# A three-sublayer decoder block on one core: the last pair's output sum, norm and store in two halves, and a new table of starting places for the order

## The chip, the cores and the metric

One Trainium2 chip, one of its cores, one launch. The metric is the device time in microseconds (us) of one execution. All arithmetic is in float32.

## The reference

A batch of 16 sequences of 256 tokens with 256 channels goes through three sublayers, each added to its input and layer-normed:

```python
x = _layernorm(x + attn(x, ...))        # scan-type attention: projections, conv, sin/cos, cumsums
x = _layernorm(x + xattn(x, ctx, ...))  # auto-correlation: DFT of q and k, top-5 lags, roll of v
x = _layernorm(x + ffn(x, ...))         # two branches of 8 experts with a router
```

In the last one, with `xV = Q @ V_k`, `cum_yW = cumsum(K @ W_k)` along the tokens and router weights `w`:

```python
out = einsum('btkr,kdr->btd', xV * cum_yW * w[..., None], U) + w @ b
out = out / n_valid                      # then fwd + alpha * inv, times W_O.T
```

## The kernel before, in words

The 16 sequences are worked on in 8 pairs. For each pair the program lists seven stages: `front` (in-projection, convolution, gates), `body` (sin, cos, cumulative sums, out-projection, first norm), `context` and `back` (keys and values of the second sublayer, kept in HBM between the two), `attention` (second sublayer and norm), `router` and `experts` (third sublayer). `fold_weights` multiplies weights with each other once, ahead of the pairs (`w_ps`).

No instruction is issued as it is listed. Class `Later` records every call as an `Op`; then `Work.run` lays out an order for all five engines, and `Work.give` issues it. So nearly all instructions carry the one line L452, and table loads of ScalarE L450. The layout is a list schedule: each engine takes, of the operations that can go, the one with the lowest rank. It is made three times (`PASSES`). In the first pass a rank is `place(part)`, which is `begin[pair] + part * length` of the stage's row in the table `PLACES`; in the next passes it is the latest start found by going back through the layout before. The shortest of the three layouts by the planner's own costs is issued. `Work.note` finds which operation must wait for which; for PSUM, the memory that TensorE writes, `Work.box` takes a bank as a whole: two operations on different columns of one bank are taken to meet.

```python
    def place(stage, pair, part):
        length, *begin = PLACES[stage]
        return begin[pair] + part * length
```

A change of a few numbers in `PLACES`, or of the list of operations, can thus move instructions of all pairs on all engines.

`experts(p)`: eight expert blocks make `e` (128 x 512: 128 rows, 2 x 256 tokens) from two matmul groups `c_ps` and `v_ps`; the router's weights come in as `wb` through a DMA. Then `u_ps`: for each token half `c` (tokens 0 to 127, then 128 to 255) and each sequence `j` of the pair, 8 matmuls with `u_o` and one with the bias `b_o`. There are two banks, `banks[j]`, one for each sequence; columns 0 to 255 of a bank hold half `c = 0`, columns 256 to 511 half `c = 1`. At the end VectorE adds each bank to `x` (128 x 512), `layernorm` takes four tiles of 128 x 256 (statistics on VectorE, square root and scaling on ScalarE), and GpSimd issues one store of 256 KB for each sequence.

Names in the profile: `sc_ps`, `in_ps` belong to `front`; `y`, `ss`, `out_ps` to `body`, `sn` and `cs` being its sine and cosine tiles; `dft_ps` on `bothc` and `kv_ps` to `context`; `dft_ps` on `dx`, `q_ps`, `corr_ps`, `w_t_ps`, `w_f_ps`, `roll_ps`, `wo_ps` to `attention`; `fx_ps`, `h_ps`, `l_ps`, `lt_ps`, `wt_ps` to `router`.

Of the kernel before, what the change touches and what calls it, by code (L numbers as in the profile page):

```python
# [16 lines left out]
ALU = mybir.AluOpType  # L17
# [4 lines left out]
P = 128  # L22
# [10 lines left out]
NP = B // 2  # L33
# [3 lines left out]


PLACES = {
    "front": (1.0, 1.75, 3.7, 4.05, 4.2, 5.15, 5.65, 6.15, 8.0),  # L40
    "body": (0.5, -1.2, 1.45, 3.3, 1.4, 4.5, 4.55, 6.85, 7.75),
    "ctx": (0.9, 2.18, 0.8, 1.3, 1.6, 1.9, 1.3, 1.55, 2.55),
    "back": (0.5, -2.85, -2.95, -4.9, -5.5, -1.75, -3.0, -1.2, 2.1),
    "att": (0.1, -1.95, -2.75, -2.4, -4.5, -0.05, 0.45, 1.4, 4.15),
    "router": (1.45, 0.9, -3.2, 2.15, 2.1, 2.9, 4.65, 5.9, 4.9),
    "expert": (1.18, 4.05, 3.55, 5.65, 5.85, 7.4, 6.9, 9.8, 12.25),
    "fold": (2.75, 2.21),
}
EARLY, SLABS, XT_BUFS, ZC_BUFS, KBUFS, VBUFS, X_BUFS = 3, 17, 1, 4, 2, 3, 9
AHEAD = range(1, NP)  # L50
# [63 lines left out]
class Work:  # L114
# [67 lines left out]
    @staticmethod  # L182
# [3 lines that stand above are left out]
# [270 lines left out]
def decoder_kernel(ctx: ExitStack, tc: tile.TileContext, a: dict, out: bass.AP):  # L456
    nc = tc.nc
    ctx.enter_context(tc.manual_schedule())
    work = Work(0.1)
    work.scalar = nc.scalar  # L460
    work.shares.update({"raw": 11, "inv": 2, "ks": 6, "ct": 2, "bothc": 1, "specc": 2, "e": 8, "wb": 3, "h": 2, "lT": 1, "lg8": 1, "fwT": 2, "x": 3, "dx": 2, "x2": 4})
    V, S, G, T, Y = (
        Later(work, name, eng)
        for name, eng in (
            ("DVE", nc.vector), ("ACT", nc.scalar), ("POOL", nc.gpsimd), ("PE", nc.tensor), ("SP", nc.sync)
        )
    )
# [7 lines left out]
    ff = ctx.enter_context(tc.tile_pool(name="ff", bufs=1))  # L475
# [13 lines left out]
    def new(pool, shape, tag, bufs=1, name=None):  # L489
        work.apart()  # L490
        return pool.tile(shape, F32, name=name or tag, tag=tag, bufs=bufs)

    def slab(shape, name):
        return new(ff, shape, "slab", SLABS, name)
# [4 lines left out]
    def f_bank(name):  # L499
        return new(f_ps, [P, 512], "fps", 4, name)  # L500

    def split(ps, n=2):
        return ps.rearrange("p (c d) -> p c d", c=n)
# [70 lines left out]
    def layernorm(pool, tag, tiles, eps=None):  # L574
        n = len(tiles)
        st = new(pool, [P, n, 6], tag + "st")
        mv = new(pool, [P, n, 2], tag + "mv")
        rs = new(pool, [P, 3, n], tag + "rs")
        for i, t in enumerate(tiles):
            V.bn_stats(st[:, i, :], t)  # L580
            V.bn_aggr(mv[:, i, :], st[:, i, :])
        t, y, nb = (rs[:, i, :] for i in range(3))
        S.activation(t, mv[:, :, 1], AF.Sqrt, bias=b_eps if eps is None else eps)
        V.reciprocal(y, t)
        V.scalar_tensor_tensor(nb, mv[:, :, 0], -1.0, y, ALU.mult, ALU.mult)
        for i, t in enumerate(tiles):
            S.activation(t, t, AF.Identity, scale=y[:, i : i + 1], bias=nb[:, i : i + 1])
# [196 lines left out]
    ps = f_bank("bv_ps")  # L784
# [362 lines left out]
    def copies(wT, kb):  # L1147

        return wT.rearrange("(n k) t -> n k t", k=KEXP)[:, kb].unsqueeze(1).to_broadcast([16, 8, 512])

    def experts(p):
        place = lambda f: work.place("expert", p, f)
        xT, cT = inputs.pop(p)
        pair = (xs[2 * p], xs[2 * p + 1])
        es = []
        for kb in range(8):
            cut = slice(kb * P, (kb + 1) * P)
            work.rank = place(kb * 0.08)
            early = kb < EARLY
            e = slab([P, 512], "e")  # L1160
            if not early:
                wb = slab([P, 512], "wb")
                Y.dma_start(out=wb, in_=copies(routed[p], kb))
            ps = f_bank("c_ps")
            for c in range(2):
                T.matmul(ps, w_c[:, c, cut], cT[:, c, :, :], start=c == 0, stop=c == 1)
            if early:
                S.copy(e, ps)
            else:
                V.tensor_tensor(e, wb, ps, ALU.mult)  # L1170
            ps = f_bank("v_ps")
            for c in range(2):
                T.matmul(ps, w_v[:, c, cut], xT[:, c, :, :], start=c == 0, stop=c == 1)
            V.tensor_tensor(e, e, ps, ALU.mult)
            es.append(e)
        wT = routed.pop(p)
        for kb in range(EARLY):
            wb = slab([P, 512], "wb")
            Y.dma_start(out=wb, in_=copies(wT, kb))
            V.tensor_tensor(es[kb], es[kb], wb, ALU.mult)  # L1180
        banks = [None, None]
        for c in range(2):
            for j in range(2):
                work.rank = place(0.65 + 0.1 * c + 0.05 * j)
                if c == 0:
                    banks[j] = f_bank("u_ps")
                work.apart()
                o, cut = banks[j][:, c * D : (c + 1) * D], slice((2 * j + c) * P, (2 * j + c + 1) * P)
                for n, i in enumerate([*range(EARLY, 8), *range(EARLY)]):
                    T.matmul(o, es[i][:, cut], u_o[:, i, :], start=n == 0, stop=False)  # L1190

            work.apart()
            work.joins = True
            for j in range(2):
                rows, cut = slice(64 * j, 64 * j + 64), slice((2 * j + c) * P, (2 * j + c + 1) * P)
                T.matmul(banks[j][:, c * D : (c + 1) * D], wT[rows, cut], b_o[rows, :], start=False, stop=True)
            work.joins = False
            work.apart()
        tiles = []
        for j in range(2):  # L1200
            V.tensor_tensor(pair[j], pair[j], split(banks[j]), ALU.add)
            tiles += [pair[j][:, 0, :], pair[j][:, 1, :]]
        work.rank = place(1.0)
        layernorm(ff, "fl", tiles)
        for j in range(2):
            G.dma_start(out=out[2 * p + j].rearrange("(c p) d -> p c d", p=P), in_=pair[j])

    fold_weights()
    for p in range(NP):
        for stage in (front, body, context, back, attention, router, experts):  # L1210
            stage(p)
# [138 lines left out]
```

## Time and profile before

| what | us |
|---|---|
| median of 3 timed runs (lowest, highest) | 867.02 (865.38, 867.68) |
| the profiled execution, its own time | 862.73 |
| its span, first to last instruction | 861.0 |
| TensorE busy in it | 811.5 |
| VectorE busy | 695.2 |
| ScalarE busy | 596.2 |
| GpSimd busy | 254.3 |

The profiled execution is one execution; its time holds 1.73 us outside the span. Busy time of TensorE (PE) is that of pipelined matmuls whose ends are modelled; PEld is its weight load; DVE is VectorE, ACT ScalarE, POOL GpSimd, SP the engine that issues most DMAs. The span falls into three parts: a beginning (to about 55 us) in which weights are fetched, folded and the first pair's chain starts; a long middle in which two to three pairs are under way at once; and an end, from about 785 us, in which only the last pair's `router` and `experts` are left.

### The profile page before, as it was taken

To read this page: it belongs to the slowest core of one execution; us is meant where nothing else is said; L and a number is where in the kernel's file an instruction comes from. 1 tells how busy PE (TensorE), PEld (TensorE's weight loads), DVE (VectorE), ACT (ScalarE), POOL (GpSimd) and SP (SyncE) were. 2 spreads that over 40 slices of the span, in tenths; PEclk is the share of its full clock that TensorE was granted. 3 is DMA by queue.
4 is the path that set the end of the run, shared out by engine and by line. 5 is a ranking of instruction groups with operands and counts; after the bars stand their busy time and mean duration, and the time that the engine had idled before them with its cause. 6 is when DMAs were issued, how large, how long until landed. Compare 5 with 4: busy or idle time off the path is not lost.

```text
span 861.0 us, 12052 instructions
## 1 busy us (share of the span) xinstructions
PE 811.5 (94%) x4180; PEld 462.2 (54%) x4180; DVE 695.2 (81%) x1200; ACT 596.2 (69%) x874; POOL 254.3 (30%) x301
## 2 busy tenths in 40 slices
PE   4779998999989999999998999999999999999994
PEld 1336564564546654764453746655457357548453
DVE  6479799879899999999999799988979994472431
ACT  2769968699897999599668956769388932712601
POOL 8501456551512132433220312434122111221000
PEclk9879999999999999999999999999999999999997
DMA  7952787374745336535484436336351711130040
GB/s 232 346 129 51 191 246 200 124 198 111 187 105 143 81 87 168 130 71 142 100 181 96 116 78 146 106 86 158 76 133 39 186 34 50 44 80 1 24 98 25
DMA packets 57421, 103.30 MB, mean 120 GB/s; under 512 B 7616, under 2 KB 24032, under 8 KB 57360
## 3 DMA queue, kind: packets, MB, share of 16 engines
q1 hardware_dynamic: 47760, 71.85, 35.6%
q0 software_dynamic: 9600, 30.69, 10.9%
q8 instruction: 33, 0.54, 0.3%
q14 instruction: 28, 0.23, 0.1%
HBM read 28.06 MB, written 11.53 MB: 46 GB/s over the span
## 4 chain that ended last, share of the span: by engine, by line
PE 63%; ACT 13%; DVE 9%; issue 6%; DMA 5%; POOL 2%; SPq 1%; POOLq 0%; DVEq 0%; ACTq 0%
PE u_ps L452 11%; PE v_ps L452 9%; PE c_ps L452 9%; PE h_ps L452 5%; PE kv_ps L452 4%; PE in_ps L452 4%; PE w_ps L452 3%; PE wo_ps L452 3%; ACT L450 3%; DVE cs L452 3%; PE y L452 2%; ACT cs L452 2%; PE ss L452 2%; PE out_ps L452 2%; DVE sn L452 2%
## 5 line engine op out<-in xcount | busy, mean ns | idle before, releaser
L450 ACT ACT_TABLE_LOAD x101 | 129.6, 1283 | 1.8
L452 PE MATMUL v_ps<-fxT,w_v 128*128 128x512 f32 x256 | 121.0, 602 | 2.6 <-DVE e L452 1.2
L452 PE MATMUL c_ps<-fcT,w_c 128*128 128x512 f32 x256 | 120.1, 601 | 0.1
L452 PE MATMUL u_ps<-u_o,e 128*128 128x256 f32 x512 | 116.4, 382 | 0.0
L452 PEld LDWEIGHTS u_ps<-u_o,e 128*128 128x128 f32 x512 | 95.6, 190 | 19.1 <-issue 6.7
L452 DVE TENSOR_TENSOR_SCAN cs<-again,cs 128x1024 f32<-128x1024 bf16 x32 | 77.3, 2417 | 0.0
L452 PEld LDWEIGHTS v_ps<-fxT,w_v 128*128 128x128 f32 x256 | 46.2, 190 | 54.1 <-issue 42.8
L452 DVE TENSOR_TENSOR_SCAN sn<-again,sn 128x1024 f32<-128x1024 bf16 x32 | 74.6, 2332 | 0.1
L452 PEld LDWEIGHTS c_ps<-fcT,w_c 128*128 128x128 f32 x256 | 46.5, 190 | 50.2 <-issue 46.8
L452 DVE SCALAR_TENSOR_TENSOR zc<-in_ps,pv,zc 128x510 f32<-128x510 f32 (+2 forms) x96 | 69.3, 734 | 1.6 <-ACT zc L452 1.1
L452 PE MATMUL h_ps<-fxT,w_h 128*128 128x512 f32 x128 | 61.4, 619 | 4.0 <-ACT fxT L452 4.0
L452 PE MATMUL in_ps<-xT,in_proj_w 128*128 128x512 f32 x128 | 62.6, 619 | 2.0 <-DVE sc L452 2.0
L452 PE MATMUL kv_ps<-Wkv,specc 128*128 128x512 f32 x128 | 61.3, 612 | 3.2 <-ACT specc L452 2.9
L452 POOL TENSOR_TENSOR pp<-qf,kf 128x256 f32<-128x256 f32 (+1 forms) x32 | 43.7, 1383 | 69.3 <-ACT qf L452 64.7
L452 DVE TENSOR_TENSOR e<-e,v_ps 128x512 f32<-128x512 f32 x64 | 43.0, 674 | 14.5 <-PE v_ps L452 14.4
L452 POOL DMA_DIRECT2D out<-x x16 | 11.7, 730 | 135.5 <-ACT x L452 123.1
L452 ACT ACTIVATE sn<-sn,theta_col 128x512 f32<-128x512 f32 x64 | 44.6, 714 | 9.0 <-DMA sn<-zc 8.8
L452 POOL TENSOR_TENSOR t<-vf,wf 128x256 f32<-128x256 f32 x32 | 22.8, 732 | 92.0 <-ACT wf L452 49.7
L452 DVE SCALAR_TENSOR_TENSOR cs<-cs,sn 128x1024 f32<-128x1024 f32 x32 | 42.1, 1315 | 9.3 <-ACT cs L452 9.1
L452 DVE TENSOR_TENSOR sn<-sn,ge 128x1024 f32<-128x1024 f32 x32 | 41.4, 1295 | 6.6 <-ACT sn L452 3.7
L452 ACT ACTIVATE ge<-sn 128x1024 f32<-128x1024 f32 x32 | 33.7, 1053 | 17.0 <-DVE sn L452 9.6
L452 ACT ACTIVATE zc<-in_ps,pv 128x512 f32<-128x512 f32 x32 | 24.6, 778 | 30.1 <-PE in_ps L452 30.1
(220 smaller groups left out, 1600.5 us busy)
## 6 DMA issues: line engine op xcount, KB each, us to landing
sn<-zc SPq DMA_DIRECT2D x64, 256.0 KB
ge<-g SPq DMA_DIRECT2D x64, 256.0 KB
wb<-fwT SPq DMA_DIRECT2D x64, 256.0 KB
ct<-in_ctx SPq DMA_DIRECT2D x16, 256.0 KB
xT<-in_xT SPq DMA_DIRECT2D x8, 512.0 KB
x<-in_x POOLq DMA_DIRECT2D x16, 256.0 KB, 3.9
ph<-sc SPq DMA_DIRECT2D x64, 64.0 KB
gate<-zc SPq DMA_DIRECT2D x64, 64.0 KB
```

The lines of the kernel that those rows point to most:

```text
L450: self.scalar.preload_act_table_set(self.TABLES[table])
L452: call(*args, **kw)
```

## The change

Two things. In `experts`, for the last pair alone (`p == NP - 1`), the add, the layernorm and the store are listed once for each token half, right behind that half's matmuls, on 128 x 256 tiles; the other pairs keep one add, norm and store behind both halves, now with the adds ranked at `place(1.0)` too. And all eight rows of `PLACES` have other numbers.

```diff
 PLACES = {
-    "front": (1.0, 1.75, 3.7, 4.05, 4.2, 5.15, 5.65, 6.15, 8.0),
-    "body": (0.5, -1.2, 1.45, 3.3, 1.4, 4.5, 4.55, 6.85, 7.75),
-    "ctx": (0.9, 2.18, 0.8, 1.3, 1.6, 1.9, 1.3, 1.55, 2.55),
-    "back": (0.5, -2.85, -2.95, -4.9, -5.5, -1.75, -3.0, -1.2, 2.1),
-    "att": (0.1, -1.95, -2.75, -2.4, -4.5, -0.05, 0.45, 1.4, 4.15),
-    "router": (1.45, 0.9, -3.2, 2.15, 2.1, 2.9, 4.65, 5.9, 4.9),
-    "expert": (1.18, 4.05, 3.55, 5.65, 5.85, 7.4, 6.9, 9.8, 12.25),
-    "fold": (2.75, 2.21),
+    "front": (1.05, 1.75, 3.2, 4.1, 4.35, 5.8, 5.7, 6.05, 8.5),
+    "body": (0.6, -1.0, 1.65, 3.5, 1.75, 4.5, 3.85, 6.75, 8.2),
+    "ctx": (0.85, 2.88, 0.0, 2.0, 2.15, 4.15, 1.95, 2.15, 3.45),
+    "back": (2.6, -3.7, -2.4, -4.8, -5.75, -1.4, -2.85, -2.3, 2.85),
+    "att": (2.1, -6.05, -6.25, -7.35, -9.0, -5.1, -2.85, -2.25, 2.15),
+    "router": (1.15, 2.5, -2.35, 3.8, 3.2, 4.25, 5.1, 7.65, 5.65),
+    "expert": (0.98, 4.45, 3.9, 5.85, 5.8, 8.3, 7.75, 9.95, 13.3),
+    "fold": (4.45, 2.76),
 }
...
             work.joins = False
             work.apart()
-        tiles = []
-        for j in range(2):
-            V.tensor_tensor(pair[j], pair[j], split(banks[j]), ALU.add)
-            tiles += [pair[j][:, 0, :], pair[j][:, 1, :]]
-        work.rank = place(1.0)
-        layernorm(ff, "fl", tiles)
-        for j in range(2):
-            G.dma_start(out=out[2 * p + j].rearrange("(c p) d -> p c d", p=P), in_=pair[j])
+
+            if p == NP - 1 or c == 1:
+                halves = [c] if p == NP - 1 else [0, 1]
+                work.rank = place(1.0)
+                for j in range(2):
+                    x, ps = pair[j][:, halves[0] : c + 1, :], split(banks[j])[:, halves[0] : c + 1, :]
+                    V.tensor_tensor(x, x, ps, ALU.add)
+                layernorm(ff, "fl", [pair[j][:, h, :] for j in range(2) for h in halves])
+                for j in range(2):
+                    rows = out[2 * p + j].rearrange("(c p) d -> p c d", p=P)[:, halves[0] : c + 1, :]
+                    G.dma_start(out=rows, in_=pair[j][:, halves[0] : c + 1, :])
```

## The prediction

> **What bounds the kernel now.** I read the page's busy times and slices first, then TensorE's waits, then the end's timeline, then the first 75 us engine by engine. Busy times and slices, one digit for 21.5 us:
>
> ```profile
> PE 811.5 (94%) x4180; PEld 462.2 (54%) x4180; DVE 695.2 (81%) x1200; ACT 596.2 (69%) x874; POOL 254.3 (30%) x301
> PE   4779998999989999999998999999999999999994
> DVE  6479799879899999999999799988979994472431
> PEclk9879999999999999999999999999999999999997
> ```
>
> TensorE is the bound: 811.5 of 861.0 us, full from the fourth slice to the last but one. Both orders hold the same matmuls, so the time can only fall by what TensorE idles (49.5 us) or does at a lower clock. VectorE is nearly full too from about 220 to 460 us, and has room after 700. TensorE's waits, with total, count and longest in us:
>
> ```profile
> PE sc_ps L452 <- DMA xT<-in_xT: 15.7, 2, 8.8
> PE h_ps L452 <- ACT fxT L452: 4.0, 2, 3.1
> PE w_ps L452 <- ACT vf L452: 3.4, 1, 3.4
> PE kv_ps L452 <- ACT specc L452: 2.9, 2, 1.9
> PE w_f_ps L452 <- ACT wT L452: 2.0, 1, 2.0
> PE wt_ps L452 <- POOL lg L452: 1.8, 1, 1.8
> ```
>
> All waits of this view sum to 37.7 us; the other 11.3 us are the end, from TensorE's last matmul (849.70) to 861.0. Its timeline:
>
> ```profile
> 841.90 7.17 PE L452 MATMUL u_ps<-u_o,e 128*128 128x256 f32 x32
> 849.00 0.70 PE L452 MATMUL u_ps<-b_o,fwT 64*128 64x256 f32 x4
> 849.73 1.28 DVE L452 TENSOR_TENSOR x<-x,u_ps 128x512 f32<-128x512 f32 x2 [14.58 <-PE u_ps L452]
> 850.94 0.74 DVE L452 BATCH_NORM_STATS2 flst<-x 128x6 f32<-128x256 f32 x2
> ...
> 853.52 2.07 ACT L452 ACTIVATE x<-x,flrs 128x256 f32<-128x256 f32 x4 [0.44 <-DVE flrs L452]
> 854.90 0.72 POOL L452 DMA_DIRECT2D out<-x  x1 [39.09 <-ACT x L452]
> 855.89 0.72 POOL L452 DMA_DIRECT2D out<-x  x1 [0.26 <-ACT x L452]
> ```
>
> Nothing overlaps TensorE here: add, statistics, scaling, store, in that order. The sum below is made against the profiled execution's 862.73 us; the median of the timed runs is 4.3 us above it, and I carry the difference over unchanged.
>
> **Part 1, the end.** From the last matmul to the second store's issue before: 849.70 to 855.89, 6.19 us. For the last half after: two adds of 128x256 for 0.75 (the bias add of that shape took 0.42, and the second overlaps), two statistics instead of four (1.74 us for the group, so 0.87), the square root chain 0.84 as before, two scalings instead of four, the first store after one of them (0.52 + 0.35), the second 0.98 behind it, the spacing of the two stores above. 0.75 - 0.04 + 0.87 + 0.84 + 0.87 + 0.98 = 4.27. Gain 1.9; GpSimd's issue, not ScalarE, sets it. The last store moves 128 KB instead of 256 KB; at the 351 to 359 GB/s that the DMA view shows for the old ones, 0.3 less. Together **-2.2** (bounds -2.6, if stores do not space, to -1.2, if only adds and statistics shrink). The first half's chain, some 5.2 us with its stores, lies beside the 7.87 us of matmuls of the second half; without that cover it would give back all of this. Only two more stores on GpSimd's queue come of it, with nothing queued behind.
>
> The Trainium skill (DMA: Bandwidth & Descriptors, Anatomy of one DMA) fits a store from GpSimd as a fixed 2.0 us and bytes over 436 GB/s; by it halving the bytes saves an estimated 0.3 us and the rest of the landing stays, which the trace's rates agree with.
>
> **Part 2, a new wait at the end.** Both halves of a sequence lie in one bank and the planner takes a bank as a whole, so in the built program the second half's first matmuls wait for VectorE's add of the first. Queued behind it on TensorE are the second half's 36 matmuls, and the whole end. No row shows it. Lower bound: the add's 0.42 plus the 0.03 by which an add follows its matmul, 0.45. Upper: that plus a window at half clock, 1.7, so 2.2. The two waits of 0.64 and 0.91 us near 680 us left the clock at 1.00, so I take **+0.5**.
>
> **Part 3, the beginning.** The orders part after 13 matmuls. Before, TensorE waited 6.91 us for the second pair's `xT`, which SP had issued at 36.45 behind `ge` and `ph`; 3.44 for a ScalarE copy of `vf`; 1.05 for `f_dft`. After, SP issues that `xT` and all of `ph` ahead of `ge`, and GpSimd the folding weights ahead of `f_dft` and `Wkv`: these 11.4 us can go. But the first pair's chain then decides. VectorE ended its fourth scan at 59.1 us and TensorE used it at 61.6: only 2.5 us of room. TensorE has 3.4 us more work placed ahead of it (rows' durations). Against that, `ge` now stands on SP behind one `gate` copy, whose source ScalarE finished at 34.2 us: it goes out some 6.6 us later (28.2 to 34.8), of which 4.7 come back since VectorE no longer waits 4.68 us for the second `ph`. -2.5 - 3.4 + 1.9 = -4.0 if all of it lasts, 0 if the work placed ahead only leaves less for later waits. I take the middle, **-2**; bounds -6 and +4 (`ge` late by 6.6 with 2.5 of room).
>
> **Part 4, the middle.** The changed table moves instructions on all engines; only TensorE's last 292 matmul calls of 2154 stand as before, some 131 us of work. I counted, in both built orders, how much matmul work (0.86 us for a pair of 128x512, 0.43 for 128x256, and so on from the rows) stands between a group and the group that needs its result; little work between is a wait. From `fx_ps` to `h_ps`, pairs 1 to 7: 0.9, 0.9, 2.1, 0.0, 1.7, 1.8, 2.2 before, never under 1.7 after; the 0.0 is the 3.1 us wait. From `w_t_ps` to `w_f_ps`: lowest 0.0 before (the 2.0 us wait), 1.7 after. From `lt_ps` to `wt_ps`, pairs 1 to 6: lowest 6.1 before (the 1.8 us wait), 9.7 after. So 4.0 + 2.0 + 1.8 = 7.8 us go. After the 3.1 us wait the clock was low:
>
> ```profile
> 452.00:455.00 3.00, 0.59 (x5) 0.35 (x3) 2.97 (x3) 3.00 (x5) 0.00 (x0) 1.00 0.92 273
> 455.00:458.00 3.00, 2.33 (x3) 1.08 (x4) 3.00 (x3) 2.98 (x5) 0.00 (x0) 0.63 0.00 0
> ```
>
> (the first figure behind the comma is TensorE's busy time, the third from the end the granted clock). 0.37 x 3.0 = 1.1 us more. The Trainium skill (TensorE: Matmul & The Clock Gate, Part 1) puts the clock back to half only after an idle window of about 3.4 us; by that this wait of 3.08 us would have cost no clock and the sum would lack the 1.1, but the row shows 0.63, so the trace does not agree.
>
> New waits: from `dft_ps` to `kv_ps` five of 16 places have under 1 us after (one of them in the beginning), one before. The two waits there cost 2.9 us, 1.44 each; four give 5.8, so +2.9. From `dft_ps` on `dx` to `q_ps` one place has 0.9 instead of at least 1.7: +0.9, as long as the 0.9 us wait at an `h_ps` with 0.9 between. Together -7.8 - 1.1 + 3.8 = **-5.1** (bounds -10, no new wait, to +4, all old waits replaced).
>
> ScalarE has 14 table loads fewer (88 for 102, the first load included), 18.0 us by the row's 1283 ns. ScalarE is idle 265 us, so I count them at nothing beside the waits above; that is a rival's matter.
>
> **Part 5, VectorE in the middle.** By rows' durations the order after has 2 to 7 us (mean 4.8) more VectorE work ahead of the scans that feed `y` of the third and fourth pair, while TensorE's work ahead is the same within 0.4 in the mean. Before, the last three `y` groups of the third pair followed their scans by 0.0 to 0.8 us (one scan ends at 249.6, its `y` starts at 249.68). The 4.7 us that VectorE no longer waits for `ph` nearly cover it: **+0.1** (bounds 0 and +7).
>
> **Sum.** -2.2 + 0.5 - 2.0 - 5.1 + 0.1 = -8.7 us: 862.73 becomes 854.0 for a profiled execution, and the median 867.02 becomes **858.3**. A measurement of this kernel can tell about 0.3%, 2.6 us, from no change.
>
> **Rivals.** *VectorE takes over (slower).* Between 220 and 460 us VectorE is busy 97%; each wait that TensorE loses then comes back at `y`, nothing is kept of parts 3 and 4, and the scan with most work ahead sets the delay, 7.3 x 0.92 = 6.7 us (my VectorE durations add to 757 for 695 busy). 6.7 - 1.7 = +5.0: 872.0. It decides if VectorE's idle time ahead of 240 us, 44 us now, falls by less than about 2. For it: the gaps of 0.0 to 0.8. Against: the `ph` stall, and 12 of the 14 loads saved lie ahead of the first pair's last norm, so VectorE should wait less for ScalarE early.
>
> *Only the end counts.* Waits in the middle are traded one for one, as the new places at `kv_ps` suggest: -2.2 + 0.5, 865.3, no change to be told.
>
> *Table loads matter.* Line L450 has 3% of the chain that ended last, 25.8 us for 101 loads, 0.26 each; 14 fewer give -3.6 on top of the sum: 854.7. For it: several loads lie in the chain between 140 and 260 us. Against: part 4 has counted some of these waits already.
>
> **Numbers.** The forecast gets 0.55, with its own range 853 to 864; table loads 0.15; only the end 0.10; VectorE 0.20. Faster by over 0.3% is the first two, 0.70; the same 0.10; slower 0.20. The range goes from 850 (part 3 at its best under the table loads) to 871.5, just short of the rival's 872.0; some 2 in 10 stay outside.
>
> **What would show it.** Right: the last matmul to the end of the span 9.1 us instead of 11.3, a TensorE wait on VectorE's add of about 0.5 between the halves, `sc_ps` on `xT` waiting only once for long, no wait of over 1 us at `h_ps`, `w_f_ps`, `wt_ps`. Wrong: waits of `y` on `cs` or `sn` that add up to over 5 us, a long wait for `ge` before the first `y`, or a clock below 1.00 in the last 8 us of matmuls.

## The result, and the profile after

| | median, us (lowest, highest) | ratio to before, 95% |
|---|---|---|
| before, in this comparison | 866.53 (865.38, 867.68) | |
| the changed kernel | 861.80 (860.40, 862.63) | 0.9957 [0.9939, 0.9975] |
| the changed kernel, in the next comparison | 862.10 (860.64, 866.17) | 0.9977 [0.9960, 0.9994] |

So the change is faster, by 0.2 to 0.4%: by the ratios 3.7 us in the first comparison (the medians differ by 4.7) and 2.0 us in the second (before's median there: 864.54, of 35 executions). The forecast was 8.7 us, 1.0%. The two profiled executions show less still: 862.73 us before, 862.63 after, spans 861.0 and 860.8. Executions of one kernel differ here by more than the effect (before: 861.3 to 869.3 us in those 35), so single traces are used below for where TensorE waits, and medians for what it is worth.

Busy times and slices of the changed kernel, one digit for 21.5 us:

```profile
PE 810.6 (94%) x4180; PEld 463.0 (54%) x4180; DVE 698.5 (81%) x1204; ACT 580.6 (67%) x861; POOL 267.6 (31%) x303
PE   4598999899979999999999989999999999999995
DVE  5589689988999999999989989998888894563341
PEclk9899999999999999999999999999999999999998
```

TensorE's work is unchanged and so, nearly, is its idle time. Its waits (total, count, longest, in us):

```profile
PE sc_ps L452 <- DMA xT<-in_xT: 18.0, 2, 9.1
PE y L452 <- DVE cs L452: 3.6, 5, 1.5
PE kv_ps L452 <- DVE ks L452: 3.4, 1, 3.4
PE kv_ps L452 <- ACT specc L452: 3.3, 2, 1.9
PE y L452 <- DVE sn L452: 2.9, 1, 2.9
PE wt_ps L452 <- POOL lg L452: 1.4, 1, 1.4
PE c_ps L452 <- DVE x L452: 1.2, 1, 1.2
```

The view sums to 41.0 us, against 37.7 before. The rows that the prediction wanted gone are gone (`h_ps`, `w_f_ps` but 0.2 us, `w_ps` on `vf`) except `wt_ps`, and the rows above on `y`, on `ks` and on `x` are new or longer. Between 62 us and the last half of matmuls, counting waits of 0.25 us and more, 15.1 us before became 17.3. The end:

```profile
843.73 0.75 DVE L452 TENSOR_TENSOR x<-x,u_ps 128x256 f32<-128x256 f32 x2 [6.85 <-PE u_ps L452]
844.21 7.17 PE L452 MATMUL u_ps<-u_o,e 128*128 128x256 f32 x32 [0.51 <-DVE x L452]
851.31 0.70 PE L452 MATMUL u_ps<-b_o,fwT 64*128 64x256 f32 x4
852.04 0.75 DVE L452 TENSOR_TENSOR x<-x,u_ps 128x256 f32<-128x256 f32 x2 [5.90 <-PE u_ps L452]
855.39 1.07 POOL L452 DMA_DIRECT2D out<-x  x2 [7.19 <-ACT x L452]
```

From TensorE's last matmul (852.01) to the end of the span it is 8.8 us, 11.3 before; the second half waits 0.51 us for VectorE's add of the first. That is 2.0 us gained, where Parts 1 and 2 had 1.7 (-2.2 and +0.5). But the last matmul itself comes at 852.01 instead of 849.70: beginning and middle together lost 1.8 us in this execution, the 0.51 us apart.

### The profile page after: what moved, and what is told of

The parts are those of the page before. It is cut to its first block, busy times and chain, and to the rows that moved or that the text cites. A ratio compares the mean times of both kernels' runs of the same rounds, so it can differ in the third digit from the quotient of the medians.

```text
span 860.8 us, 12074 instructions
## 1 busy us (share of the span) xinstructions
PE 810.6 (94%) x4180; PEld 463.0 (54%) x4180; DVE 698.5 (81%) x1204; ACT 580.6 (67%) x861; POOL 267.6 (31%) x303
## 4 chain that ended last, share of the span: by engine, by line
PE 66%; DVE 11%; issue 7%; ACT 7%; DMA 6%; POOL 1%; SPq 1%; POOLq 0%; DVEq 0%; ACTq 0%
PE u_ps L452 12%; PE v_ps L452 10%; PE c_ps L452 9%; PE h_ps L452 5%; PE kv_ps L452 4%; PE in_ps L452 4%; PE out_ps L452 3%; PE wo_ps L452 3%; PE q_ps L452 3%; DVE cs L452 3%; PE y L452 2%; PE dft_ps L452 2%; DVE sn L452 2%; PE ss L452 2%; DMA ge<-g 2%
## 5 line engine op out<-in xcount | busy, mean ns | idle before, releaser
L452 PE MATMUL c_ps<-fcT,w_c 128*128 128x512 f32 x256 | 120.6, 603 | 2.0 <-DVE x L452 1.2
L452 PE MATMUL v_ps<-fxT,w_v 128*128 128x512 f32 x256 | 119.9, 600 | 0.0
L452 PE MATMUL u_ps<-u_o,e 128*128 128x256 f32 x512 | 116.8, 382 | 0.5 <-DVE x L452 0.5
L452 PEld LDWEIGHTS u_ps<-u_o,e 128*128 128x128 f32 x512 | 95.5, 190 | 19.4 <-issue 6.0
L452 DVE TENSOR_TENSOR_SCAN cs<-again,cs 128x1024 f32<-128x1024 bf16 x32 | 79.2, 2475 | 0.0
L452 PEld LDWEIGHTS c_ps<-fcT,w_c 128*128 128x128 f32 x256 | 47.1, 191 | 57.2 <-issue 47.7
L452 DVE TENSOR_TENSOR_SCAN sn<-again,sn 128x1024 f32<-128x1024 bf16 x32 | 75.2, 2351 | 0.1
L452 PEld LDWEIGHTS v_ps<-fxT,w_v 128*128 128x128 f32 x256 | 46.7, 190 | 52.0 <-issue 45.5
L452 DVE SCALAR_TENSOR_TENSOR zc<-in_ps,pv,zc 128x506 f32<-128x506 f32 (+2 forms) x96 | 69.7, 734 | 3.4 <-ACT zc L452 2.8
L452 PE MATMUL kv_ps<-Wkv,specc 128*128 128x512 f32 x128 | 63.4, 630 | 6.7 <-DVE ks L452 3.4
L452 PE MATMUL in_ps<-xT,in_proj_w 128*128 128x512 f32 x128 | 63.4, 622 | 2.1 <-DVE sc L452 2.1
L452 POOL TENSOR_TENSOR pp<-qf,kf 128x256 f32<-128x256 f32 (+1 forms) x32 | 46.8, 1482 | 46.7 <-ACT qf L452 43.0
L452 PE MATMUL h_ps<-fxT,w_h 128*128 128x512 f32 x128 | 59.3, 601 | 0.1
L452 DVE TENSOR_TENSOR e<-e,v_ps 128x512 f32<-128x512 f32 x64 | 42.9, 674 | 15.4 <-PE v_ps L452 15.3
L452 POOL TENSOR_TENSOR t<-vf,wf 128x256 f32<-128x256 f32 x32 | 22.2, 714 | 97.1 <-ACT wf L452 51.6
L452 DVE TENSOR_TENSOR sn<-sn,ge 128x1024 f32<-128x1024 f32 x32 | 44.2, 1382 | 8.3 <-DMA ge<-g 5.3
L452 POOL TENSOR_TENSOR g<-g,zc 128x512 f32<-128x512 f32 x16 | 24.8, 1550 | 82.4 <-ACT g L452 82.4
L452 ACT ACTIVATE sn<-sn,theta_col 128x512 f32<-128x512 f32 x64 | 44.8, 715 | 7.6 <-DMA sn<-zc 7.5
L452 ACT ACTIVATE ge<-sn 128x1024 f32<-128x1024 f32 x32 | 33.8, 1056 | 22.6 <-DVE sn L452 13.6
L452 POOL DMA_DIRECT2D out<-x x18 | 12.5, 693 | 116.8 <-ACT x L452 116.5
L452 ACT ACTIVATE sq<-cs 128x1024 f32<-128x1024 f32 x32 | 33.8, 1055 | 17.1 <-DVE cs L452 16.5
```

The lines of the kernel that those rows point to most:

```text
L452: call(*args, **kw)
```

## The experiments

All but after_again and before_again, which are the two kernels unchanged, hold the order of the instructions fixed: the list that the planner issued is written into the kernel, and parts of it are changed. (Their instructions then carry the line L588 instead of L452.) "Old order" is that of before, "new order" that of the changed kernel.

```diff
-    work.run(PASSES)
+    work.give([work.ops[int(k)] for k in ORDER], None)
```

### The two halves of the change, each alone, and both kernels again

split_alone: old order, end in halves. order_alone: new order, whole end.

```diff
-ORDER = old order, one add, norm and store at the end
+ORDER = old order up to the last pair's adds, then the halves  # split_alone
+ORDER = new order up to there, one add, norm and store         # order_alone
```

> The order of the kernel before, kept instruction by instruction; only the last pair's add, norm and store are done in two halves. If the end is worth what the two profiles show (last matmul to end of the span 11.3 us before, 8.8 after, and a new wait of 0.5 us): 2.0 us faster than before. If the measured 4.7 us come mostly from the split: 4 us or more. If the end counts for nothing: within 0.5 us of before.

> The order of the changed kernel, kept instruction by instruction; the last pair's add, norm and store are one piece as before. If the new order is worth the rest of the measured 4.7 us: 2.7 us faster than before. If VectorE takes over what TensorE no longer waits for (TensorE's waits add up to 41.0 us in the changed kernel's profile, 37.7 in the old one's): the same as before or up to 3 us slower. If the prediction's parts 3 to 5 hold: 7 us faster.

> The changed kernel once more, for the spread of its executions: if its profiled execution (860.8 us of span) was an ordinary one, another profile has a span of 859 to 861 and the same waits within 1 us each.

> The kernel before once more: its profiled execution took 862.73 us, its timed ones 865.38 to 867.68. If the profiled one was a lucky one, this profile has a span of 864 to 866 and some waits are longer than in the first; if profiled executions are faster than others as such, the span is again 861.

| run | median, us | ratio to before, 95% |
|---|---|---|
| split_alone | 863.29 | 0.9988 [0.9972, 1.0005] |
| order_alone | 864.68 | 1.0003 [0.9985, 1.0021] |
| after_again | 862.10 | 0.9977 [0.9960, 0.9994] |
| before_again | 863.42 | 0.9986 [0.9970, 1.0002] |

Before against itself comes out at 0.9986, so 0.14% is what one such comparison may be off, and split_alone's 0.9988 can't be told from it. Read as a square of medians, the halves are worth 0.1 us in the old order (before_again to split_alone) and 2.6 in the new one (order_alone to after_again); the order costs 1.3 us with the whole end and gains 1.2 with the halves. So the order alone is worth nothing that can be told, where 7 us were forecast, and the halves agree with the 2.0 us of the traces without showing them. That is the outcome of the rival *only the end counts*. The long waits repeat: the 3.39 us at `kv_ps` and the 2.90 at `y` were 3.44 and 2.90 in after_again.

### Is VectorE's load what makes the new waits?

Both kernels leave out two of the convolution's three taps on the gate groups, so they compute something else; their times show what that much less work on VectorE is worth.

```diff
             convolve(zc, split(ps), m)
+            if m >= 2:
+                work.ops[-3].parts, work.ops[-2].parts = [], []
             zcs.append(zc)
```

> The changed kernel, its order kept, with two of the three taps of the convolution left out for the two gate groups of each pair: 32 VectorE instructions of 0.73 us, 23.5 us spread over the kernel and off the chain that feeds y. If VectorE has become what ends TensorE's waits in the middle (waits on VectorE of 12 us between 60 and 850 us in the changed kernel's profile): 6 to 10 us faster than the changed kernel, and the waits of y on cs and sn and of kv_ps on ks under 3 us in all. If these waits only stand in for others: within 2 us of the changed kernel.

> The same 32 instructions left out in the order of the kernel before, with the split end. Its waits in the middle are mostly on ScalarE (h_ps, kv_ps, w_f_ps), on VectorE only 2 us. If the bound has moved to VectorE with the new order: at most 2 us faster than the split alone. If VectorE binds both orders alike: as much faster as in the new order.

new_light took 861.99 us, 0.9969 [0.9951, 0.9986], old_light 861.79, 0.9970 [0.9948, 0.9992]. VectorE was busy 679.9 us in new_light instead of 698.5, and the long waits did not move: the kernel came out 0.1% from after_again, and old_light 0.2% from split_alone, within the intervals. TensorE's timeline of new_light at the third pair's last `y`:

```profile
253.24 0.64 PE L588 MATMUL y<-sn,w_ri 128*32 128x256 f32 x8 [2.90 <-DVE sn L588]
255.42 1.08 PE L588 MATMUL y<-cs,w_ri 128*32 128x256 f32 x8 [1.54 <-DVE cs L588]
```

Both waits are to 0.01 us those of the changed kernel (252.74 and 254.92). So *VectorE takes over* falls as a matter of how much VectorE has to do. That the place of a few instructions in its queue matters is tried further down.

### Do bytes bound the beginning?

```diff
 GpSimd
-loads Wq, correlation and roll tables, out_proj_w, three x, then the raw weights
+the raw weights (all but the last five in new_late, old_late; all in new_later), then those nine loads
```

> The changed kernel, its order kept but for nine loads on GpSimd's queue (2.2 MB that nothing reads before 95 us: Wq, c_corr, c_mean, f_roll, c_roll, out_proj_w, three x), put behind the folding weights. If the beginning is bound by what the 16 DMA engines can move (busy 97% between 20 and 45 us), the second xT lands some 6 us earlier than 42.9 and the kernel is 3 to 6 us faster. If the first pair's chain on VectorE and ScalarE sets it: under 1.5 us faster.

> The same nine loads moved in the order of the kernel before, with the split end. If DMA binds the beginning of both orders: 3 to 6 us faster than the split alone, which is 1 to 2 us faster than before. If the old order's beginning is bound elsewhere (its second xT is issued as late as 36.5 us behind ge and ph): under 1.5 us.

> The changed kernel, order written out, with the same nine loads of new_late (2.2 MB: Wq, the DFT correlation and roll tables, out_proj_w, three x) moved behind the last raw weight, so that GpSimd issues them at about 60 us and they really leave the first 46 us, in which the 16 DMA engines are 97 to 100% busy. If bytes bound the beginning, 2.2 MB at some 370 GB/s let xT, ge and the raw weights land up to 5.9 us earlier and the waits of sc_ps on xT fall: about 857 to 859. If the first pair's chain bounds it, no change: 862, ratio 0.997. If the late loads are then missed (out_proj_w is first needed at about 90 us by the planner), slower by the wait.

new_late 865.0 us, 1.0005 [0.9990, 1.0020]; old_late 862.52, 0.9975 [0.9955, 0.9995]; new_later 861.56, 0.9965 [0.9950, 0.9979]: none is clearly faster than its kernel without the move, and new_late is rather slower than the changed kernel (its first two `y` wait 2.86 and 1.87 us for VectorE). In new_late and old_late GpSimd still issued the nine loads at 27 to 44 us, inside the busy beginning, so these two do not answer the question; in new_later it issued them at 52 to 58 us, and something did move. TensorE's timeline of the changed kernel:

```profile
42.92 1.94 PE L452 MATMUL sc_ps<-xT,w_sc 128*32 128x256 f32 x16 [9.07 <-DMA xT<-in_xT]
50.47 1.99 PE L452 MATMUL w_ps<-raw 128*128 128x256 f32 x8 [1.32 <-DVE bo L452]
```

and of new_later:

```profile
37.86 1.94 PE L588 MATMUL sc_ps<-xT,w_sc 128*32 128x256 f32 x16 [5.91 <-DMA xT<-in_xT]
47.87 3.56 PE L588 MATMUL w_ps<-raw 128*128 128x256 f32 x8 [3.90 <-DVE bo L588]
```

and VectorE's:

```profile
45.22 2.28 DVE L588 TENSOR_TENSOR_SCAN sn<-again,sn 128x1024 f32<-128x1024 bf16 x1
47.42 0.40 DVE L588 TENSOR_TENSOR bo<-bo,bv_ps 128x256 f32<-128x256 f32 x1
```

`xT` now comes at 37.86 instead of 42.92, and the 5.06 us are lost again within 40: `w_ps` waits 3.90 (1.32 in the changed kernel) for VectorE to read `bv_ps` out of its bank, and then takes 3.56 us for 8 matmuls (1.99), so that half of the lead is gone at 47.87 (50.47 in the changed kernel), and all of it at the `y` of 77.07 (76.74). `bv_ps` had been ready since about 32 us; the 0.40 us instruction that reads it stands in VectorE's queue behind two multiplications, which waited for `ge` till 42.94, and a scan.

### Moving single instructions past the waits

The same pattern is behind the longest new wait in the middle. The changed kernel's timeline, TensorE:

```profile
172.70 3.51 PE L452 MATMUL kv_ps<-Wkv,specc 128*128 128x512 f32 x4 [3.39 <-DVE ks L452]
```

and VectorE:

```profile
167.59 1.81 DVE L452 TENSOR_TENSOR t<-t 128x256 f32<-128x256 f32 x2
169.33 2.91 DVE L452 TENSOR_TENSOR_SCAN cs<-again,cs 128x1024 f32<-128x1024 bf16 x1
172.16 0.39 DVE L452 TENSOR_TENSOR ks<-kv_ps,b_dc 128x256 f32<-128x256 f32 x1
```

In new_ks (below) the same copy runs at 168.03, so the bank was full by then at the latest; here `ks`, which empties it, stands behind these 4.6 us of other work. And TensorE pays twice. The stretches of 3 us around the wait, with the granted clock as third figure from the end:

```profile
171.00:174.00 3.00, 1.30 (x2) 0.81 (x3) 3.00 (x5) 1.06 (x1) 2.67 (x3) 0.74 0.17 63
174.00:177.00 3.00, 3.00 (x19) 0.91 (x22) 0.52 (x1) 0.75 (x2) 0.18 (x1) 0.69 0.48 175
```

The first two runs moved several operations each, on their own engine (six in new_mend and five in old_mend, where the expectations speak of nine and six):

```diff
 new_mend (new order)
+VectorE: ks ahead of t, t, scan cs                (kv_ps, 172.70)
+VectorE: two scans ahead of t, t                  (y, 252.74)
+ScalarE: specc ahead of u_o, u_o, zc              (kv_ps, 82.48)
+ScalarE: specc ahead of ks, wf, ks                (kv_ps, 164.72)
+TensorE: u_ps ahead of wt_ps                      (wt_ps, 496.22)
 old_mend (split_alone)
+ScalarE: fxT, fxT ahead of cs, cs, zc, zc         (h_ps, 457.10)
+ScalarE: wT ahead of cs, ge                       (w_f_ps, 247.75)
+ScalarE: specc ahead of ge, sn                    (kv_ps, 152.19)
+TensorE: v_ps ahead of wt_ps                      (wt_ps, 409.53)
```

> The changed kernel with its order written out and nine single operations moved by a few places on their own engine, each ahead of a wait of TensorE in the middle: VectorE's copy ks ahead of t and a scan (the 3.39 us wait of kv_ps at 172.70), the two t multiplications behind the two scans of the third pair (2.90 + 1.54 at y, some 1.0 of it), ScalarE's specc copies ahead of copies of u_o, zc and ks (1.94 at 82.48, 1.3 of it; 1.37 at 164.72, 1.0 of it), and TensorE's next u_ps group ahead of wt_ps (1.40 at 496.22). If the new waits in the middle are what the change's gain was lost to, and each costs its own length, these 3.4 + 1.0 + 1.3 + 1.0 + 1.4 = 8.1 us go: about 854, ratio 0.988 to the kernel before. If waits in the middle only stand in for each other (what one group no longer waits, a later one does), at most 2 us go: 860 or more, ratio above 0.995.

> The order of before with the end in halves (split_alone), and six single operations moved by a few places: ScalarE's two copies fxT ahead of two activations of cs (h_ps, 3.03 at 457.10, 2.4 of it), its copy wT ahead of cs and ge (w_f_ps, 1.97 at 247.75, 1.7 of it), its copy specc ahead of ge and sn (kv_ps, 2.41 at 152.19), and TensorE's next v_ps group ahead of wt_ps (1.79 at 409.53). If each old wait cost its own length, as the prediction's 7.8 us have it, 2.4 + 1.7 + 2.4 + 1.8 = 8.3 us go: about 855 beside split_alone's 863.3, ratio about 0.989. If they stand in for each other, at most 2 us go: 861 or more.

new_mend: 857.82 us, 0.9927 [0.9904, 0.9950], 4.3 us less than after_again, half of the 8.1. old_mend: 864.37, 0.9988 [0.9971, 1.0005], the very ratio of split_alone: nothing of the 8.3. TensorE's waits in old_mend:

```profile
PE l_ps L588 <- ACT h L588: 5.2, 1, 5.2
PE y L588 <- DVE cs L588: 3.3, 2, 1.8
PE w_t_ps L588 <- ACT ks L588: 2.4, 1, 2.4
PE h_ps L588 <- ACT fxT L588: 0.7, 1, 0.7
```

The 3.03 at `h_ps` is 0.67 and `l_ps`, the next group of the same chain, waits 5.22 (0.87 in split_alone), for `h`, which ScalarE makes at 464.63 at the end of a queue that leaves it no gap from 455.80 on, so sending `fxT` ahead did not bring `h` forward; the 2.41 at `kv_ps` is 2.37 at `w_t_ps` 3 us later, for a bank that ScalarE empties; the 1.79 at `wt_ps` and 1.97 at `w_f_ps` became 0.9 more and 1.48 at `y`. In all, split_alone waits 16.6 us in the middle, old_mend 17.6 (counted as above). The next runs part new_mend's moves, and take the beginning's bank:

```diff
+VectorE: ks ahead of t, t, scan cs                         # new_ks: this alone
+new_mend without that move                                 # new_rest
+new_later; VectorE: bo<-bo,bv_ps ahead of sn, cs, scan sn  # new_bo
+new_mend without the wt_ps move; new_bo;
+VectorE: x<-x,u_ps ahead of t, t, sc (c_ps, 506.74)        # new_best
```

> The changed kernel with one single operation moved: VectorE's copy ks, which empties the bank that kv_ps waits 3.39 us for at 172.70, stands ahead of two t multiplications and a scan instead of behind them. In new_mend this wait was gone and nothing came in its place, and the clock, 0.74 and 0.69 in the two stretches of 3 us behind it, stayed at 1.00. If this one copy carries what new_mend gained: 3.4 for the wait and 0.26 x 3 + 0.31 x 3 = 1.7 for the clock, about 857 to 859, ratio 0.992 to 0.994. If the eight other moves carry it, no more than 862, ratio 0.997.

> new_mend without that one move: the eight others (t behind the scans, specc twice, u_ps ahead of wt_ps). Theory after new_mend's trace: a wait for the last link of a chain over several engines comes back at the next group of the chain, so these give nothing: about 862, ratio 0.997. If each wait cost its own length, 8.1 - 3.4 = 4.7 us less than the changed kernel, about 857.

> new_later and one single operation moved: VectorE's bo<-bo,bv_ps, which empties a bank that w_ps waited 3.90 us for (47.87 in new_later), stands ahead of the first pair's sn, cs and scans instead of behind the first scan. If that bank is what kept the 2.2 MB from paying, w_ps goes 3.9 us earlier, y then waits for the first cosine scan some 1.5 to 2.5, and the second y comes 1.5 to 3.5 us earlier: about 858 to 860. If the first pair's chain on VectorE ends the beginning, no change to new_later, 861.6.

> All moves that the traces speak for: new_mend without u_ps ahead of wt_ps, VectorE's add of x ahead of two t multiplications and sc (the wait of c_ps for it, 1.15 us), and the beginning of new_bo. If gains at banks add up: new_mend's 857.8, less some 1 for the add and 1.5 to 3.5 for the beginning, about 853 to 855, ratio 0.987 to 0.989. If the beginning gives nothing, 857, ratio 0.992.

| run | median, us (lowest, highest) | ratio to before, 95% |
|---|---|---|
| new_ks | 859.00 (858.57, 859.89) | 0.9942 [0.9924, 0.9960] |
| new_rest | 863.46 (860.96, 865.99) | 0.9992 [0.9977, 1.0007] |
| new_bo | 859.90 (858.98, 860.90) | 0.9949 [0.9929, 0.9970] |
| new_best | 855.66 (854.97, 856.47) | 0.9903 [0.9883, 0.9923] |

One instruction of 0.41 us, moved by some 4 us, carries what can be told of new_mend's gain: new_ks is 3.0 us below after_again by the ratios. The five other moves together give nothing (new_rest), but one of them, `u_ps` ahead of `wt_ps`, seems to have done harm: with it `c_ps` waits 2.8 us for VectorE's add of `x` (new_mend and new_rest), without it 1.2 (new_ks), and the clock in new_rest is 0.76 and 0.67 in the two stretches of 3 us from 504 to 510. That may hide a small gain of the other four. TensorE's timeline of new_ks:

```profile
170.41 1.98 PE L588 MATMUL kv_ps<-Wkv,specc 128*128 128x512 f32 x4 [0.73 <-ACT specc L588]
172.32 0.64 PE L588 MATMUL y<-sn,w_ri 128*32 128x256 f32 x8
```

and VectorE's:

```profile
168.03 0.41 DVE L588 TENSOR_TENSOR ks<-kv_ps,b_dc 128x256 f32<-128x256 f32 x1
168.37 1.48 DVE L588 TENSOR_TENSOR t<-t 128x256 f32<-128x256 f32 x2
169.77 2.89 DVE L588 TENSOR_TENSOR_SCAN cs<-again,cs 128x1024 f32<-128x1024 bf16 x1
```

`y` starts at 172.32 instead of 176.14, 3.8 us earlier; the clock between 170 and 179 is 1.00; and 3.0 of the 3.8 us are left at the last half of `u_ps` (841.25 instead of 844.21). Nothing comes back at `y`, and the scan that `ks` went ahead of ends only 0.4 us later than before the move: TensorE had been waiting for room, not for a result.

In new_bo the bank is free when `w_ps` comes; its second `y` starts at 57.59 instead of 61.33 (60.30 in new_later), and the last half of `u_ps` at 841.63, 2.6 us earlier. By the medians new_bo can't be told from new_later (0.9949 and 0.9965, intervals overlapping), and no run moved `bo` without also moving the nine loads. new_best adds the two places: its last half starts at 837.27, 6.9 us earlier than in the changed kernel, it is 3.4 us below new_ks by the ratios, and 0.9903 is 8.4 us of 863.6. Its add of `x` also went ahead to free a bank, and gave nothing: `c_ps` waits 0.77 instead of 1.15, and the next `v_ps` 0.83 that it had not waited. new_best is the fastest version of this study.

## Why the prediction was right and wrong

**Parts 1 and 2 (-2.2, +0.5)** held: 8.8 us after the last matmul where 9.1 was forecast, 0.51 us for the add, clock 1.00 in the last matmuls. Part 1 alone came to 2.5 us instead of 2.2, inside its bounds: from the last matmul to the second store's issue it is 3.9 us instead of the 4.27 worked out, since the two stores were issued 0.53 apart and not 0.98, and from there to the end 0.2 less than before. (128 KB at the 351 to 359 GB/s named there is 0.37 us, not 0.3; the stores of 128 KB landed 2.0 us after their issue where the two of 256 KB took 2.6.)

**Part 3 (-2.0)** was nothing by the traces: up to 62 us TensorE's waits sum to 22.5 us before and 22.5 after. The wait for `vf` and that for `f_dft` went as foreseen, but TensorE waited for `xT` twice for long (8.92 and 9.07, not once): SP issued the second `xT` at 28.2 instead of 36.5, and with the DMA engines 99% busy between 20 and 45 us TensorE started on it 4.5 us earlier, not 8, with less to do till then. new_later shows what would have come next: `xT` 5 us earlier is worth nothing while `bv_ps` holds its bank until VectorE's first scan is done. The working had looked at transfers and at the scans, and at no bank.

**Part 4 (-5.1)** is the term that failed, and its step is the one on new waits. Of its -7.8, 6.2 us went at the places named (`h_ps` and `w_f_ps`; `wt_ps` kept 1.40). But new waits were sought only where little matmul work lies between two groups (`kv_ps` on `specc`, `q_ps`: +2.9 and +0.9 forecast, +0.4 and nothing measured). The 3.39 us at `kv_ps` on `ks`, with the clock lost behind it, is of another kind: the bank's earlier user is read late. Counting matmul work from producer to consumer can't show that; it is the consumer on VectorE, and what is queued ahead of it, that had to be followed. new_ks shows this one wait to be worth 3.0 us. The 2.90 and 1.54 at `y` were in the views of Part 5 and put at 0.1; what they cost was not shown, since moving two `t` out of their way took no more than 0.8 off the two together (new_rest), in a kernel that came out no faster.

A second step is in doubt: each old wait was counted at its own length. old_mend takes 8.3 us of the old order's waits off by other means and gains nothing, because later groups wait instead. But if the old waits had been worth nothing in the new order too, that order would have come out some 3 us slower than the old one for its `ks` wait alone, and it came out even. With that wait mended, new_ks lies 4.0 us below split_alone by the ratios, where the prediction had 7.0 for Parts 3 to 5. How the missing 3.0 us divide between the old waits, the `y` waits and the beginning stays open.

**Part 5 (+0.1)** asked whether VectorE's load matters. It does not (new_light), but the `y` waits summed to 6.5 us, over the 5 that the prediction set as a sign of being wrong. VectorE's queue ahead of the longest of them:

```profile
246.34 0.75 DVE L452 TENSOR_TENSOR t<-vf,w_f_ps 128x256 f32<-128x256 f32 x2 [0.18 <-ACT wf L452]
247.01 1.66 DVE L452 TENSOR_TENSOR sn<-sn,ge 128x1024 f32<-128x1024 f32 x1
248.60 0.75 DVE L452 TENSOR_TENSOR t<-t 128x256 f32<-128x256 f32 x2
249.27 1.21 DVE L452 TENSOR_TENSOR cs<-cs,ge 128x1024 f32<-128x1024 f32 x1
250.40 2.28 DVE L452 TENSOR_TENSOR_SCAN sn<-again,sn 128x1024 f32<-128x1024 bf16 x1
252.60 2.26 DVE L452 TENSOR_TENSOR_SCAN cs<-again,cs 128x1024 f32<-128x1024 bf16 x1
```

The `y` of 252.74 starts when the first scan ends, and that of 254.92 when the second does: TensorE waits there for results.

**The rivals.** *Only the end counts* is what happened in the sum, and its reason, waits traded for waits (15.1 us in the middle became 17.3), fits; the place that it named, `kv_ps` on `specc`, does not. *Table loads matter*: 14 fewer (87 in the row of L450 where 101 stood) and 18 us less of ScalarE came with the new order, whose 1.0003 shows no gain; no run changed the loads alone. *VectorE takes over* had the right places, `y` and VectorE, and the wrong reason.

**The base.** The sum was made against one execution 4.3 us under its median, and this offset was carried over. The changed kernel's profiled execution lay 0.8 above its median. With a spread of 8 us between executions of before, such an offset says nothing of the next kernel.

**The clock.** By the Trainium skill (TensorE: Matmul & The Clock Gate, Part 1) an idle window of about 3.4 us puts the clock back to half. Here the granted clock fell behind shorter waits too. Behind waits of 2.90 and 1.54 us with 0.5 us of small matmuls between them the trace has 0.72, 0.50 and 0.64 in three stretches of 3 us (253 to 262), and behind a single wait of 1.94 us, that of `kv_ps` on `specc` at 82.48, it has (the clock third from the end):

```profile
82.00:85.00 3.00, 2.52 (x5) 1.11 (x6) 2.85 (x3) 3.00 (x5) 2.85 (x2) 0.78 0.00 0
85.00:88.00 3.00, 3.00 (x9) 1.07 (x11) 1.85 (x3) 2.61 (x5) 0.37 (x1) 0.65 0.00 0
```

There 8 matmuls took 5.40 us, and 3.70 at 164.72; before, 4 took 3.34 behind the wait of 1.94 at 151.54, and 1.98 behind that of 0.94 at 140.68. Length alone does not decide: 1.97 us at 248.75 before, and 1.40 and 1.15 us after, left 1.00. So the prediction's 1.1 us for one place was right to go by the row, but its 1.44 us for each wait of `kv_ps` on `specc` left out a clock that can cost as much again.

## What to carry to other kernels

Ask of each wait whether the engine waits for a result or for room. A wait for a bank whose content was ready long ago can be a short instruction standing behind long ones in the emptying engine's queue. Here, moving that one instruction took the wait and the clock lost behind it away at one bank (new_ks), seems to have done so at a second (new_bo) and gave nothing at a third (`x`); the moves at waits for a result gained nothing that could be told, since a later group waited instead (old_mend) or the wait shrank little (new_rest). And when a new order removes waits that the old trace shows, look for those that it makes: an order's gain is a difference of two sums of like size.

## What was not expected of the hardware

In the changed kernel's trace ten of the 64 sine and cosine scans of 128x1024 on VectorE took 2.47 to 5.06 us (2.91 at 169.33), the others 2.26 to 2.29. All ten had elementwise work of GpSimd beside them for part of their time, but that alone does not do it: others, like that of 608.62, had it beside them all through and took 2.28. The two `t<-t` of 128x256 took 1.81 us at 167.59 and 0.75 at 248.60 with GpSimd at rest. This stretched the queue ahead of `ks`; what decides it stays open. And executions of one and the same program differ by up to 1.3% (859.99 to 871.13 us in the second set of 35), although the long waits in the middle repeat within 0.1 us.
